# Tying gathers to the instruction queue of VectorE: a mark and a copy, or a pass over the gathers' own index columns

## The chip, the cores and the metric

The kernel runs on one core of a Trainium2 chip. The core has five engines with a queue each, which run side by side and wait for one another through semaphores: TensorE (PE in the profile, its weight loads PEld), VectorE (DVE), ScalarE (ACT), GpSimd (POOL) and SyncE (SP), which here only issues transfers. The metric is the device time of one launch in microseconds. Three runs before the change took 3876.13, 3902.46 and 3901.21 us; their median is 3901.21 us. The execution that was profiled took 3892.48 us, with a span of 3890.7 us.

## The reference

There are 16 graphs of 1024 nodes with 64 channels, and a weighted 1024 by 1024 adjacency for each, with some 16 neighbours to a node. Four graph layers follow one another, each applied to `relu(layernorm(x))` and added to `x`. Layers 0, 1 and 3 are matrix products with the adjacency and small weights. Layer 2 is the one that matters here: it thins the neighbourhood of every node by a rule on the ranks of its neighbours, and takes, for every node and channel, a weighted sum of three quantiles over the neighbours that are left:

```python
vals = where(valid[..., None], x[:, None, :, :], big)
sv = sort(vals, axis=2)                      # over the neighbours of a node
for tau, wt in zip([0.25, 0.5, 0.75], [0.25, 0.5, 0.25]):
    pos = clip(tau * (m - 1), 0)             # m neighbours
    lo, hi, frac = floor(pos), ceil(pos), pos - floor(pos)
    agg = agg + wt * (gather(lo) * (1 - frac) + gather(hi) * frac)
```

Two small products, a relu and the node mask follow.

## The kernel before

**Stages.** The function `direct_path` is cut into streams, which are Python generators over the 16 graphs. `adjacency` loads a graph, transposes it on TensorE and makes sort keys of the neighbours. `neighbour_lists` reads the keys back, sorted by the number of neighbours, and takes from each row the largest eight again and again (line 1111 and lines 1120 to 1127), until it has a list of row numbers for every node. `layers` does layers 0 and 1 and stores the rows of layer 2 in DRAM, as `h_d`. `gathers` fetches, for each place of each list, one row of 64 numbers per node. `sorts` runs a sorting network over the fetched rows on VectorE (line 1316) and forms the weighted sum (lines 1333 and 1335). `tail` fetches the results back into the order of the nodes (line 1355) and does the rest.

**Batches and groups.** The 1024 nodes of a graph are ordered by their number of neighbours and cut into eight batches of 128, one node to a partition. `PLACES` gives the number of places of each batch, 21 down to 11, and `LISTS` the length of its list in the tile `index`, 40 down to 16 columns; the lists lie one behind another. `GROUPS` takes the batches in five groups: the first two batches alone, the others in pairs, whose rows lie side by side in one tile `raw`, so that one step of the network sorts both. The few long lists of the first batch are packed and fetched separately (line 1264).

**Gathers.** A gather is one indirect transfer that GpSimd prepares: 128 rows of `h_d`, chosen by one column of `index`, into one place of `raw` (line 1283). There are 124 of them for a graph, 1984 in all. GpSimd works through its queue in order; apart from the gathers it has only the key loads (line 1096), the packed rows and the results to fetch, and the gate's copies.

**The order.** All is emitted by hand in one pass over the streams, under a plan: a `Clock` holds estimated times of the engines, each stream says by `yield` at what estimated VectorE time it wants to go on, and the loop at the end of the function takes the next stream whose time has come. So the order of the instructions in every queue is fixed when the program is built. The plan counts 1.39 us for a gather, and lets GpSimd's clock run 5 us ahead of VectorE's at most (`yield clk.pool - 5` after every four gathers).

**The gate.** That the plan puts a gather at some point of VectorE's work doesn't hold GpSimd back: its queue is its own. The function `gate` (lines 919 to 925) ties the two. At every fourth gather, and before the key loads of a graph, VectorE writes one element of `slots` (a memset, line 922), and GpSimd copies that element to `opened` (line 924). The copy waits for the memset, and what stands behind the copy in GpSimd's queue waits with it. A gate is left out when the last one lies less than 3 us back on the plan's clock. The profile has 477 of them.

Of the kernel before, what the change touches and what calls it, by code (L numbers as in the profile page):

```python
# [7 lines left out]
F32 = mybir.dt.float32  # L8
# [6 lines left out]
ALU = mybir.AluOpType  # L15
AX = mybir.AxisListType

P = 128
C = 64
NB = 8  # L20
N = 1024
# [12 lines left out]
I16 = mybir.dt.int16  # L34
# [21 lines left out]
PLACES = [21, 19, 17, 16, 15, 13, 12, 11]  # L56
PACKS, NPACK = [(0, 0, 21, 2, 64), (1, 0, 23, 1, 32), (1, 32, 24, 4, 24), (2, 0, 28, 10, 12)], 3

LISTS = [40, 24, 24, 16, 16, 16, 16, 16]
KB = 4  # L60


# [62 lines left out]
def _program(cap, low, above, homes):  # L125

    home, out = [0] * cap, []
    for layer, flips in zip(_network(cap, low, above), homes.split(), strict=True):  # L130
        pairs = sorted({(home[i], home[j]) for i, j, _, _ in layer})
        steps, moved = ([], []), []
        for (s, u), flip in zip(pairs, flips, strict=True):
            some = [c for c in layer if (home[c[0]], home[c[1]]) == (s, u)]
            for greater in (True, False):
                moves = flip in ("bi" if greater else "bj")
                to = (s if greater else u) ^ moves
                for first, dims in _patterns([(i, j) for i, j, a, b in some if (a if greater else b)]):
                    steps[0 if moves else 1].append((greater, s, u, to, first, dims))
                moved += [c[0 if greater else 1] for c in some if moves]  # L140
        for e in moved:
            home[e] ^= 1
        out += steps[0] + steps[1]
    return out, [(home[q], q, e) for e, q in enumerate(_wanted(cap, low))]
# [587 lines left out]
def direct_path(ctx: ExitStack, tc: tile.TileContext, t: dict, out: bass.AP, flag):  # L732
# [3 lines left out]
    nc = tc.nc  # L736
# [84 lines left out]
    clk = Clock()  # L821
# [90 lines left out]
        return v.rearrange("c (q u p) -> c u q p", u=2, p=P)[:, u]  # L912


    marks = []
    slots = const.tile([1, 8], F32, name="mark")
    opened = const.tile([1, 2], F32, name="gate")

    def gate():
        if not marks or clk.dve > marks[-1] + 3.0:  # L920
            k = len(marks)
            nc.vector.memset(slots[:, k % 8:k % 8 + 1], 0.0)  # L922
            clk.dve += 0.15
            nc.gpsimd.tensor_copy(opened[:, k % 2:k % 2 + 1], slots[:, k % 8:k % 8 + 1])  # L924
            marks.append(clk.dve)


    state = [dict() for _ in range(B)]
    done = set()
    queued = []  # L930
# [156 lines left out]
    def neighbour_lists(b):  # L1087


        g = state[b]  # L1090
        ks = []

        def load_keys(i):
            if i < NB:
                k = lists.tile([P, N], F16, name="k", bufs=KB)
                nc.gpsimd.indirect_dma_start(k, None, g["keys_d"],
                                             bass.IndirectOffsetOnAxis(ap=g["node"][:, i:i + 1], axis=0))
                clk.pool = max(clk.pool, clk.dve) + 1.3
                ks.append((k, clk.pool + 3.5))

        gate()
        for i in range(KB):
            load_keys(i)
        total = sum(LISTS)
        found = lists.tile([P, total], F32, name="found", bufs=1)
        m = g["m"]
        o = 0
        for i in range(NB):
            src, at = ks[i]
            yield at  # L1110
            nc.vector.max(out=found[:, o:o + 8], in_=src)  # L1111
            clk.dve += 1.15
            yield clk.dve
            less, before = src.bitcast(I16), None
            for r in range(1, LISTS[i] // 8):


                least = found[:, o + 7:o + 8]
                if r == 1:
                    ts(less, src, least, None, op0=ALU.subtract)  # L1120
                else:
                    ts(less, less, before, least, op0=ALU.add, op1=ALU.subtract)
                before = least
                most = nodes.tile([P, 8], U16, name="most")
                nc.vector.max(out=most, in_=less.bitcast(U16))  # L1125
                o += 8
                ts(found[:, o:o + 8], most.bitcast(I16), 0.0, least, op0=ALU.min, op1=ALU.add)
                clk.dve += 1.8
                yield clk.dve
            o += 8  # L1130
            load_keys(i + KB)
        index = lists.tile([P, total], I32, name="index")
        to, of = (v.rearrange("p (s u) -> p u s", u=2) for v in (index, found))
        none = lists.tile([P, total // 2], F32, tag="far", name="none", bufs=1)
        nc.vector.tensor_copy(to[:, 1], of[:, 1])
        ts(none, of[:, 0], 0.0, float(N + 1), op0=ALU.is_equal, op1=ALU.mult)
        tt(to[:, 0], none, of[:, 0], ALU.add)
        pack_d = dram.tile([NPACK, P], I32, name="pack_d")
        pack = nodes.tile([P, NPACK], I32, name="pack")
        for l, p0, s0, ns, nn in PACKS:  # L1140
            nc.sync.dma_start(pack_d[l, p0:p0 + ns * nn].rearrange("(n s) -> n s", s=ns), index[:nn, s0:s0 + ns])
        for l, size in enumerate(sizes):
            nc.sync.dma_start(pack[:size, l:l + 1], pack_d[l, :size].rearrange("(n o) -> n o", o=1))

        s = nodes.tile([P, 2, NB], F32, name="s")
        tt(s[:, 0], m, cap8, ALU.is_gt)
        tt(s[:, 1], m, low8, ALU.is_lt)
        tt(s[:, 0], s[:, 0], s[:, 1], ALU.max)
        tt(bad, bad, s[:, 0], ALU.max)


        above = nodes.tile([P, 2, NB], I32, name="above")
        ts(above[:, 0], m, 1.0, None, op0=ALU.add)
        ts(above[:, 1], above[:, 0], 1, None, op0=ALU.arith_shift_right)
        tt(s[:, 0], half8, above[:, 1], ALU.subtract)
        ts(s[:, 1], m, -1.0, None, op0=ALU.add)
        at = nodes.tile([P, 3, NB], F32, name="at")
        for k in range(3):
            nc.vector.scalar_tensor_tensor(at[:, k], s[:, 1], (k + 1) / 4, s[:, 0], op0=ALU.mult, op1=ALU.add)
        far = lists.tile([P, 3, QT], F32, name="far", bufs=1)  # L1160
        o, e = 0, E_Q
        for b0, n, cap, low, *_ in GROUPS:
            k = len(_wanted(cap, low))
            tt(far[:, :, o:o + k * n].rearrange("p t (q i) -> p t q i", i=n),
               cf[:, None, e:e + k, None].to_broadcast([P, 3, k, n]),
               at[:, :, None, b0:b0 + n].to_broadcast([P, 3, k, n]), ALU.subtract)
            o, e = o + k * n, e + k
        act(far, far, AF.Abs)
        for k, w in enumerate((0.25, 0.5, 0.25)):
            act(far[:, k], far[:, k], AF.Relu, bias=wcol[:, k:k + 1], scale=-w)  # L1170
        g.update(index=index, pack=pack)
        done.add(("index", b))
        yield after(1.7, act=1.7)
        while b >= 2 and ("sorts", b - 2) not in done:
            yield None
        wts = lists.tile([P, QT], F32, name="wts", bufs=2)
        tt(wts, far[:, 0], far[:, 2], ALU.add)
        tt(wts, wts, far[:, 1], ALU.add)
        clk.dve += 0.4
        g.update(wts=wts)  # L1180
        done.add(("lists", b))
# [65 lines left out]
    def gathers(b):  # L1247
        g = state[b]
        yield max(g["rows_at"], clk.pool)
        for k, (b0, n, cap, *_) in enumerate(GROUPS):  # L1250
# [15 lines left out]
                    clk.pool += 1.39  # L1266
                rows_d = dram.tile([NPACK, P, C], F32, name="rows_d")
            for s in range(cap):
                if s % (4 // n) == 0:
                    gate()  # L1270
                if k == 0 and s == 9:
                    for l, size in enumerate(sizes):
                        nc.sync.dma_start(rows_d[l, :size], packed[:size, l * C:(l + 1) * C])
                if k == 0 and s == 17:
                    for l, p0, s0, ns, nn in PACKS:
                        nc.sync.dma_start(raw[:nn, s0:s0 + ns, :],
                                          rows_d[l, p0:p0 + ns * nn].rearrange("(n s) c -> n s c", s=ns))
                for i in range(n):
                    if s >= PLACES[b0 + i]:
                        continue  # L1280
                    clk.pool += 1.39
                    at = sum(LISTS[:b0 + i]) + s
                    nc.gpsimd.indirect_dma_start(raw[:, s, i * C:(i + 1) * C], None, h_ds[b % 3],  # L1283
                                                 bass.IndirectOffsetOnAxis(ap=g["index"][:, at:at + 1], axis=0))
                if (s + 1) % (4 // n) == 0:
                    yield clk.pool - 5
# [128 lines left out]
    nc.vector.memset(none[:, :1], BIG)  # L1415
    nc.vector.memset(none[:, 1:], 0.0)
    sizes = [max(p0 + ns * nn for l, p0, _, ns, nn in PACKS if l == k) for k in range(NPACK)]
    programs = [_program(*group[2:]) for group in GROUPS]
    edge = lists.tile([1, 2, C], F32, tag="ab", name="edge")
    nc.vector.memset(edge[:, 0], 0.0)  # L1420
# [169 lines left out]
```

## Time and profile before

| what | before |
|---|---|
| median of three runs | 3901.21 us |
| span of the profiled execution | 3890.7 us |
| VectorE busy | 3040.5 us, 78% |
| GpSimd busy | 2650.6 us, 68% |
| TensorE busy | 2010.3 us, 52% |
| ScalarE busy | 1424.2 us, 37% |
| gathers, line 1283 | 1984, 2151.8 us |
| the gate's copies, line 924 | 477, 162.7 us |
| the gate's memsets, line 922 | 477, 27.5 us |

The profile gives for each engine the time in which it did something. A group of instructions is given as a line of the code, an engine, an operation, the tiles written and read, the count, the busy time and the mean duration of one, and the idle time of the engine just before such an instruction, with what ended it ("issue" means that nothing was waited for that the profile shows). The chain of waits is followed back from the last instruction, at each step to what released it. In the lists of instructions in order of time, the first number is the start in us, the second the duration.

### The profile page before, as it was taken

What the parts mean: (1) busy time and instruction counts of PE and PEld (TensorE: products, weight loads), DVE (VectorE), ACT (ScalarE), POOL (GpSimd) and SP (SyncE); (2) the same over time, 40 slices, a digit from 0 to 9 for tenths busy, and PEclk for the clock granted to TensorE, in tenths of its full rate; (3) what the DMA queues carried; (4) which work ended last, traced back from release to release, by engine and by line L of the source; (5) the groups of instructions that cost most, each with busy time, mean ns of one, the idle gap of its engine ahead of it and who ended that gap; (6) DMA issues with size and microseconds to landing.
All of it is one profiled execution on the core that took longest, in us unless ns stands there. A gap on an engine that the chain in (4) does not pass through costs nothing.

```text
span 3890.7 us, 30892 instructions
## 1 busy us (share of the span) xinstructions
PE 2010.3 (52%) x7587; PEld 934.0 (24%) x7587; DVE 3040.5 (78%) x7345; ACT 1424.2 (37%) x2786; POOL 2650.6 (68%) x2792
## 2 busy tenths in 40 slices
PE   6463463746554474645546565565457545641113
PEld 3222221223222222222222222232222212220101
DVE  2557877969787897888788798989699867979572
ACT  5444343244443434333342444343444424330000
POOL 1077565867767776776767677777778776777781
PEclk8676666667676686666666676767667666765555
DMA  2313233152423425233341525242343424232121
GB/s 89 124 40 117 48 98 114 47 166 53 153 64 94 121 65 152 69 114 79 86 126 48 172 54 163 58 156 56 100 119 108 113 52 126 65 105 59 43 52 55
DMA packets 237343, 362.37 MB, mean 93 GB/s; under 512 B 126848, under 2 KB 128496, under 8 KB 237152
## 3 DMA queue, kind: packets, MB, share of 16 engines
q1 hardware_dynamic: 156912, 255.00, 19.0%
q0 software_dynamic: 80096, 104.70, 13.5%
q8 instruction: 62, 1.02, 0.1%
q14 instruction: 129, 1.06, 0.1%
q10 hardware_dynamic: 144, 0.59, 0.0%
HBM read 245.30 MB, written 114.81 MB: 93 GB/s over the span
## 4 chain that ended last, share of the span: by engine, by line
DVE 42%; issue 16%; POOL 10%; PE 10%; another core or an unknown queue 9%; ACT 9%; DMA 4%; SPq 0%; DVEq 0%; ACTq 0%; POOLq 0%
DVE other L1316 11%; DVE raw L1316 10%; POOL raw L1283 8%; DVE most L1125 5%; PE pt L882 4%; DVE found L1111 2%; DVE agg L1335 2%; ACT adjt L1220 2%; ACT sink L1055 2%; DVE k L1120 1%; DMA k<-keys_d,node 1%; POOL res L1355 1%; PE pt L906 1%; DVE nb L947 1%
## 5 line engine op out<-in xcount | busy, mean ns | idle before, releaser
L1283 POOL DMA_INDIRECT raw<-h_d,index x1984 | 2151.8, 1085 | 558.9 <-issue 532.6
L1316 DVE TENSOR_TENSOR other<-raw 128x512 f32<-128x512 f32 (+11 forms) x816 | 536.8, 688 | 152.0 <-DMA raw<-h_d,index 103.6
L882 PE MATMUL pt<-adjt,ha 128*65 128x512 f32 (+1 forms) x1024 | 489.7, 640 | 63.0 <-DVE ha L1207 27.1
L924 POOL COPY gate<-mark 1x1 f32<-1x1 f32 x477 | 162.7, 341 | 409.4 <-DVE mark L922 372.6
L994 PE MATMUL pt<-eh,nbt 128*128 128x512 f16 (+3 forms) x1024 | 238.3, 381 | 322.1 <-ACT nbt L983 256.1
L954 PE MATMUL pt<-ef,a 128*128 128x128 f32 x1024 | 212.5, 367 | 294.9 <-issue 112.4
L1316 DVE TENSOR_TENSOR raw<-other 128x512 f32<-128x512 f32 (+10 forms) x464 | 355.8, 791 | 5.3
L1125 DVE MAX8 most<-k 128x8 uint16<-128x1024 uint16 x208 | 255.4, 1228 | 10.9 <-DVE k L1120 3.3
L954 PEld LDWEIGHTS pt<-ef,a 128*128 128x128 f32 x1024 | 163.4, 190 | 383.8 <-issue 186.6
L1032 ACT ACTIVATE nb<-pt 128x1024 f16<-128x1024 f32 x128 | 130.6, 1021 | 328.7 <-remote 169.3
L955 ACT COPY adjt<-pt 128x512 f32<-128x512 f32 x256 | 140.3, 585 | 282.6 <-remote 148.0
L882 PEld LDWEIGHTS pt<-adjt,ha 128*65 128x65 f32 (+1 forms) x1024 | 149.2, 149 | 386.3 <-issue 375.3
L1028 PE MATMUL pt<-eh,gone 128*128 128x128 f16 x1024 | 128.7, 255 | 181.9 <-DVE gone L1006 90.6
L1316 DVE TENSOR_TENSOR raw<-other,raw 128x640 f32<-128x640 f32 (+3 forms) x448 | 216.5, 494 | 6.7 <-remote 1.8
L994 PEld LDWEIGHTS <-nbt 128*128 128x128 f16 x1024 | 111.2, 121 | 452.8 <-ACT nbt L983 286.0
L1316 DVE TENSOR_TENSOR raw<-raw,other 128x128 f32<-128x128 f32 (+7 forms) x496 | 211.6, 436 | 6.1
L883 ACT COPY big<-pt 64x1024 f32<-64x1024 f32 (+1 forms) x32 | 32.2, 1008 | 502.5 <-PE pt L882 299.3
L961 ACT ACTIVATE nb<-nb 128x512 f16<-128x512 f16 x256 | 159.7, 629 | 147.7 <-DVE nb L947 53.8
L1392 PE MATMUL tm<-at,ha 128*64 128x512 f32 x512 | 176.8, 794 | 67.0 <-DMA at<-adjt_d 59.1
L1316 DVE TENSOR_TENSOR other<-other,raw 128x128 f32<-128x128 f32 (+4 forms) x448 | 201.6, 461 | 4.5 <-DVE other L1316 0.3
L1001 ACT ACTIVATE gone<-pt,sf 128x512 f16<-128x512 f32 x256 | 161.6, 685 | 104.7 <-remote 35.1
L1111 DVE MAX8 found<-k 128x8 f32<-128x1024 f16 x128 | 156.4, 1222 | 42.5 <-DMA k<-keys_d,node 42.4
(189 smaller groups left out, 4249.3 us busy)
## 6 DMA issues: line engine op xcount, KB each, us to landing
a<-in_adj_dram SPq DMA_DIRECT2D x64, 1024.0 KB
adjt_d<-adjt SPq DMA_DIRECT2D x64, 1024.0 KB
at<-adjt_d SPq DMA_DIRECT2D x128, 512.0 KB
keys_d<-nb SPq DMA_DIRECT2D x64, 512.0 KB
raw<-h_d,index POOLq DMA_INDIRECT x1984
x<-in_x_dram SPq DMA_DIRECT2D x16, 256.0 KB
h_d<-h SPq DMA_DIRECT2D x16, 256.0 KB
agg_d<-agg SPq DMA_DIRECT2D x16, 256.0 KB
```

Source lines behind the costliest of these rows:

```text
L882: nc.tensor.matmul(p[p0:p0 + n, s], h[:, j, :n], adjt[:, j, s], start=j == 0, stop=j == NB - 1)
L924: nc.gpsimd.tensor_copy(opened[:, k % 2:k % 2 + 1], slots[:, k % 8:k % 8 + 1])
L954: nc.tensor.transpose(p[:, u * P:(u + 1) * P], a[:, j * P:(j + 1) * P], identf)
L955: nc.scalar.copy(adjt[:, 4 * q:4 * q + 4, i * P:(i + 1) * P], p.rearrange("p (u m) -> p u m", m=P))
L961: act(nb[:, i, s], nb[:, i, s], AF.Copy, accum_out=mn[:, q, i:i + 1])
L994: nc.tensor.matmul(p[:, o:e], nbt[:, j, :], stair[:, :e - o], start=j % 4 == 0, stop=j % 4 == 3 and j != i)
L1001: act(gone[:, i, s], p[:, s], AF.Abs, bias=sf[:, 2 + q, i:i + 1], scale=2.0)
L1111: nc.vector.max(out=found[:, o:o + 8], in_=src)
L1125: nc.vector.max(out=most, in_=less.bitcast(U16))
L1283: nc.gpsimd.indirect_dma_start(raw[:, s, i * C:(i + 1) * C], None, h_ds[b % 3], bass.IndirectOffsetOnAxis(ap=g["index"][:, at:at + 1], axi ...
L1316: tt(view(two[to], *((i, vi) if greater else (j, vj)), w), view(two[s], i, vi, w), view(two[u], j, vj, w), ALU.max if greater else ALU.min)
L1392: nc.tensor.matmul(p[q * C:(q + 1) * C, :], ha[:, j, :], even(ats[j], q), start=j == 0, stop=j == NB - 1)
```

## The change

The gate goes away: no memset, no copy, no `slots`, no `opened`, and nothing in front of the key loads. In its place the wait is put on what the gather reads anyway. Before every four gathers VectorE adds zero, in place, to the four columns of `index` that these gathers will read. A gather reads its column, so it waits for the pass, without an instruction of its own on GpSimd. A pass is made for every four gathers; the rule of 3 us is gone.

For that the four columns must lie side by side. In a paired group four gathers in a row are two places of two batches, so the lists of paired batches are now interleaved, place by place; `FIRST` gives where a group begins. The lists are written with a stride of two there, the row numbers are turned into integers in two parts (single batches and pairs) in place of one, and `found`, which now has gaps where the shorter list of the first pair ends, is set to zero once and kept.

```diff
+FIRST = [0, 40, 64, 112, 144, 176]
...
-    def gate():
-        if not marks or clk.dve > marks[-1] + 3.0:
-            k = len(marks)
-            nc.vector.memset(slots[:, k % 8:k % 8 + 1], 0.0)
-            clk.dve += 0.15
-            nc.gpsimd.tensor_copy(opened[:, k % 2:k % 2 + 1], slots[:, k % 8:k % 8 + 1])
-            marks.append(clk.dve)
...
-        gate()
         for i in range(KB):
             load_keys(i)
...
+            k, n = next((k, n) for k, (b0, n, *_) in enumerate(GROUPS) if b0 <= i < b0 + n)
+            first = FIRST[k] + (i - GROUPS[k][0])
+            eights = [found[:, e:e + 7 * n + 1:n] for e in range(first, first + LISTS[i] * n, 8 * n)]
...
-                ts(found[:, o:o + 8], most.bitcast(I16), 0.0, least, op0=ALU.min, op1=ALU.add)
+                ts(eights[r], most.bitcast(I16), 0.0, least, op0=ALU.min, op1=ALU.add)
...
-        nc.vector.tensor_copy(to[:, 1], of[:, 1])
-        ts(none, of[:, 0], 0.0, float(N + 1), op0=ALU.is_equal, op1=ALU.mult)
-        tt(to[:, 0], none, of[:, 0], ALU.add)
+        for e, z, n in ((0, FIRST[2], 1), (FIRST[2], total, 2)):
+            to, of = (v[:, e:z].rearrange("p (s u i) -> p u s i", u=2, i=n) for v in (index, found))
+            less = none[:, e // 2:z // 2].rearrange("p (s i) -> p s i", i=n)
+            nc.vector.tensor_copy(to[:, 1], of[:, 1])
+            ts(less, of[:, 0], 0.0, float(N + 1), op0=ALU.is_equal, op1=ALU.mult)
+            tt(to[:, 0], less, of[:, 0], ALU.add)
...
-                if s % (4 // n) == 0:
-                    gate()
+                if s % (4 // n) == 0 and s < PLACES[b0]:
+
+                    some = g["index"][:, FIRST[k] + s * n:FIRST[k] + s * n + 4]
+                    ts(some, some, 0, None, op0=ALU.add)
+                    clk.dve += 0.15
...
-                    at = sum(LISTS[:b0 + i]) + s
+                    at = FIRST[k] + s * n + i
...
+    found = const.tile([P, FIRST[-1]], F32, name="found")
+    nc.vector.memset(found, 0.0)
```

More of the change, by code (lines that the diff above doesn't have):

```diff
@@ L912, in even @@
         return v.rearrange("c (q u p) -> c u q p", u=2, p=P)[:, u]
-    marks = []
-    slots = const.tile([1, 8], F32, name="mark")
-    opened = const.tile([1, 2], F32, name="gate")
-    def gate():
-        if not marks or clk.dve > marks[-1] + 3.0:
-            k = len(marks)
-            nc.vector.memset(slots[:, k % 8:k % 8 + 1], 0.0)
-            clk.dve += 0.15
-            nc.gpsimd.tensor_copy(opened[:, k % 2:k % 2 + 1], slots[:, k % 8:k % 8 + 1])
-            marks.append(clk.dve)
     state = [dict() for _ in range(B)]
@@ L1099, in load_keys @@
                 ks.append((k, clk.pool + 3.5))
-        gate()
         for i in range(KB):
             load_keys(i)
-        total = sum(LISTS)
-        found = lists.tile([P, total], F32, name="found", bufs=1)
+        total = FIRST[-1]
         m = g["m"]
-        o = 0
         for i in range(NB):
             src, at = ks[i]
+            k, n = next((k, n) for k, (b0, n, *_) in enumerate(GROUPS) if b0 <= i < b0 + n)
+            first = FIRST[k] + (i - GROUPS[k][0])
+            eights = [found[:, e:e + 7 * n + 1:n] for e in range(first, first + LISTS[i] * n, 8 * n)]
             yield at
-            nc.vector.max(out=found[:, o:o + 8], in_=src)
+            nc.vector.max(out=eights[0], in_=src)
             clk.dve += 1.15
@@ L1115, in neighbour_lists @@
             for r in range(1, LISTS[i] // 8):
-                least = found[:, o + 7:o + 8]
+                least = eights[r - 1][:, 7:8]
                 if r == 1:
@@ L1125, in neighbour_lists @@
                 nc.vector.max(out=most, in_=less.bitcast(U16))
-                o += 8
-                ts(found[:, o:o + 8], most.bitcast(I16), 0.0, least, op0=ALU.min, op1=ALU.add)
+                ts(eights[r], most.bitcast(I16), 0.0, least, op0=ALU.min, op1=ALU.add)
                 clk.dve += 1.8
                 yield clk.dve
-            o += 8
             load_keys(i + KB)
         index = lists.tile([P, total], I32, name="index")
-        to, of = (v.rearrange("p (s u) -> p u s", u=2) for v in (index, found))
         none = lists.tile([P, total // 2], F32, tag="far", name="none", bufs=1)
-        nc.vector.tensor_copy(to[:, 1], of[:, 1])
-        ts(none, of[:, 0], 0.0, float(N + 1), op0=ALU.is_equal, op1=ALU.mult)
-        tt(to[:, 0], none, of[:, 0], ALU.add)
+        for e, z, n in ((0, FIRST[2], 1), (FIRST[2], total, 2)):
[4 more added lines that the diff above has]
+            tt(to[:, 0], less, of[:, 0], ALU.add)
         pack_d = dram.tile([NPACK, P], I32, name="pack_d")
```

## The prediction, made before the result was known

> **What bounds the kernel now.** I read the page from the top: busy shares, then the chain of waits, then the groups and the waits of GpSimd.
>
> ```profile
> PE 2010.3 (52%) x7587; PEld 934.0 (24%) x7587; DVE 3040.5 (78%) x7345; ACT 1424.2 (37%) x2786; POOL 2650.6 (68%) x2792
> ...
> DVE 42%; issue 16%; POOL 10%; PE 10%; another core or an unknown queue 9%; ACT 9%; DMA 4%; SPq 0%; DVEq 0%; ACTq 0%; POOLq 0%
> ...
> L1283 POOL DMA_INDIRECT raw<-h_d,index x1984 | 2151.8, 1085 | 558.9 <-issue 532.6
> ...
> L924 POOL COPY gate<-mark 1x1 f32<-1x1 f32 x477 | 162.7, 341 | 409.4 <-DVE mark L922 372.6
> ```
>
> VectorE is the backbone: 78% busy, and the largest part of the chain. No engine is full, so the end is set by VectorE's work plus its waits. GpSimd comes second. Its 162.7 us of copies look like a prize of 4% of the span, and the 372.6 us in front of them like another. Neither is one as it stands: the 372.6 us is the waiting that the gate is there to cause, and it will stand before the gathers instead (124.2 us of it is the lead-in before the first keys). What the 162.7 us are worth, the order of time shows.
>
> ```profile
> 1005.10 0.95 POOL L1283 DMA_INDIRECT raw<-h_d,index  x1 [0.31 <-issue]
> ...
> 1006.05 0.18 POOL L924 COPY gate<-mark 1x1 f32<-1x1 f32 x1
> ...
> 1006.39 0.97 POOL L1283 DMA_INDIRECT raw<-h_d,index  x1 [0.16 <-issue]
> ...
> 1007.66 0.95 POOL L1283 DMA_INDIRECT raw<-h_d,index  x1 [0.30 <-issue]
> ```
>
> Two gathers in a row lie 0.30 us apart even with nothing between. A copy starts at once behind a gather, runs in that gap, and the next gather follows 0.16 us later. With VectorE idle the gate so lengthens the gap from 0.30 to 0.34 us only. Over the whole trace, 392 of the 477 copies start without a wait, and the gap around them has a mean of 0.489 us, against 0.307 us between gathers.
>
> **How far GpSimd reaches the end.** What VectorE waited for:
>
> ```profile
> DVE stat L858 <- ACT mid L856: 105.6, 11, 36.3
> DVE other L1316 <- DMA raw<-h_d,index: 103.6, 13, 25.8
> ...
> DVE found L1111 <- DMA k<-keys_d,node: 42.4, 9, 9.1
> ```
>
> Gathers hold the sorts up for 103.6 us in 13 places, key loads hold up the lists for 42.4 us. Walking the chain piece by piece, 295 gathers and 77 of the 477 copies lie on it. A copy starts on average 4.3 us after its mark: GpSimd is mostly behind its ties, and reaches the end of a group too late in some graphs only.
>
> [...] The trace agrees for copies: 0.18 us with MAX8 running on VectorE, a mean of 0.53 us when they met an `other<-raw` sort step. Gathers take 0.952 us beside an idle VectorE and 1.148 us beside sort steps. VectorE loses next to nothing: its sort steps are 0.006 us over their floor with or without a gather beside them, and small integer passes that met a gather took 0.17 us mostly, 0.4 us at the worst, never a whole gather. [...] two independent passes of 0.17 us each start 0.08 us apart (1023.90 and 1023.98).
>
> **The change, part by part.** I start from 3893 us, the mean of the four times known (3876.13, 3902.46, 3901.21, 3892.48), since the median stands at the upper end of them.
>
> Copies gone. 392 gaps shrink from 0.489 to 0.307 us: 392 x 0.182 = 71 us. At the 85 copies that did wait, the gather now waits itself; the copy (0.18 us or more) drops out, some 0.2 us each, 17 us. Together 88 us of GpSimd's queue. On the chain lie 77 copies: 77 x 0.19 = 15 us. The other copies lie where GpSimd afterwards waits for VectorE anyway.
>
> Passes in place of memsets. The built programs have 544 passes for 477 memsets. No 4-column integer pass stands in the trace. The nearest row is this, and its neighbours have 190 and 192 ns:
>
> ```profile
> L971 DVE TENSOR_SCALAR si<-si 128x8 int32<-128x8 int32 x16 | 2.9, 182 | 0.5
> ```
>
> A pass will thus be listed at 0.17 to 0.19 us, some 100 us of busy time in all. What it costs the queue is less. A memset (0.06 us, here at 1001.21) slips into the bubble between two dependent sort steps:
>
> ```profile
> 1000.77 0.49 DVE L1316 TENSOR_TENSOR raw<-raw 128x320 f32<-128x320 f32 x1
> 1001.21 0.06 DVE L922 MEMSET mark<- 1x1 f32 x1
> 1001.30 0.43 DVE L1316 TENSOR_TENSOR raw<-other,raw 128x256 f32<-128x256 f32 x1
> ```
>
> The step behind it starts 0.04 us after the one before it ended, as it does without a memset. Over all sort steps, the gap from end to next start is -0.042 us without and -0.011 us with a memset, so a memset costs 0.03 us. For a pass the bounds are 0.03 us and the listed 0.185 us; I take 0.05, since a pass is independent of both neighbours, and the next may start 0.08 us behind it. That is 544 x 0.05 - 477 x 0.03 = 13 us, with ends at 2 and 86 us. Behind a pass in the queue stand sort steps and list steps, but it waits for nothing: its columns were made by VectorE long before; only one pass in a graph also waits for the transfers that read the packed columns, issued many microseconds earlier.
>
> A pass may also hold a gather up. Gathers beside a sort step and a `tensor_scalar` took 1.271 us against 1.148 us, those beside MAX8 and a `tensor_scalar` 0.983 us; I take 0.05 us for each of 544, 27 us of GpSimd's queue, which leaves 61 of its 88 us, and by the same share of the chain 10 of the 15 us.
>
> Lists. Three conversions (0.214, 0.199, 0.248 us) become six smaller ones at about 0.2 us: 0.54 us more, 9 us over 16 graphs. The stride of two in results of eight columns I cost at nothing[...]. The one memset of `found` lies in the lead-in.
>
> Sum: VectorE's queue +22 us. Its share on the end lies between 42% (chain) and 78% (busy): 9 to 17 us, I take 13. GpSimd -10 us. That gives +3 us, 3896; of the rest, the better fit with the plan, which counts 5.56 us for four gathers where 4 x 1.085 + 3 x 0.307 + 0.489 = 5.75 us were needed (now about 5.6), should take away some of the 103.6 us of late gathers; 13 places at 0.5 us are about 7 us. I put the end at 3889 us, 0.3% under the median.
>
> **Rivals.**
> *GpSimd paces more than the chain shows.* The chain follows one last waiter; gathers that end sooner also free transfers and key loads sooner. If all 61 us reach the end and VectorE pays 10: 3893 - 61 + 10 = 3842. For it: GpSimd's lag of 4.3 us and the plan's deficit of 0.19 us for every four gathers. Against it: 85 gates at which GpSimd stood still, where what it has saved is given back.
> *Passes cost what they are listed at.* 86 + 9 = 95 us on a queue that is the backbone; all of it on the path, less 10: 3978; with half on the path, 3930. I work with 3945. For it: the passes carry 128 partitions and raise a semaphore each. Against it: the 0.08 us between independent passes.
> *The order.* The other VectorE instructions stand in another order at 311 places of the built program, key loads and result fetches move by some four gathers, and 67 more ties hold gathers that were free before. Four gathers are 5.6 us; if half the graphs lose them once: +45 us, 3935. The same shift may gain as much.
>
> **Numbers.** Within 1% of 3901 (3862 to 3940) as worked out: 0.45. GpSimd paces, or the order gains: 0.32, at 3842. The two slow rivals: 0.23 together, at 3935 to 3945. Range: 3825 leaves out only a gain beyond the first rival, 3950 the passes at nearly full price.
>
> **What will show it.** Right: GpSimd's busy time falls by about the copies' 163 us less some lengthening of gathers, to some 2500 us; the gap before a fourth gather is 0.30 us; passes are listed near 0.18 us and VectorE's busy time rises by 40 to 80 us; VectorE's waits for gathers stay at 70 to 110 us. Wrong: passes of 0.5 us or more[...], gathers at 1.15 us or more on average, or a wait before a pass; then it is slower. If the waits for gathers and keys, 146 us together, fall under 80 us, the first rival is right.

## The result, and the profile after

The changed kernel took 3998.35 us (median of 4 runs, 3985.07 to 4009.79), the kernel before 3889.51 us (4 runs, 3876.13 to 3902.46). The ratio is 1.0279, with a 95% interval of 1.0222 to 1.0336: 2.8% slower, and outside the predicted range. Ratios, here and below, are formed from the fast runs alone (at most 1.5% above the kernel's fastest), and can differ by up to 0.9% from the quotient of two medians. The profiled execution has a span of 4008.0 us.

The lines of the page that answer to those of before (busy shares; chain of waits; the gathers; below them, from the list of groups, the pass):

```profile
PE 2038.4 (51%) x7587; PEld 941.9 (23%) x7587; DVE 3077.1 (77%) x7461; ACT 1425.0 (36%) x2786; POOL 2463.3 (61%) x2315
...
DVE 40%; PE 16%; another core or an unknown queue 13%; ACT 11%; issue 10%; DMA 5%; POOL 4%; SPq 0%; DVEq 0%; ACTq 0%; POOLq 0%
...
L1274 POOL DMA_INDIRECT raw<-h_d,index x1984 | 2127.1, 1072 | 1091.2 <-issue 525.4
```

```profile
L1260 DVE TENSOR_SCALAR index<-index 128x4 int32<-128x4 int32 x544 | 89.5, 176 | 0.0
```

Every single item of the change came out about as small as it was priced. The 544 passes are listed at 176 ns, GpSimd has 187 us less to do, VectorE 37 us more, and a gather takes 1072 ns, where it took 1085. GpSimd's part of the chain fell from 10% to 4%. What grew is the rest: TensorE's part from 10% to 16%, and from 9% to 13% the part that the profile gives to "another core or an unknown queue". There is no other core here; it is time for which the profile finds no releaser. In the list of waits the same thing is called "remote". ScalarE's longest waits in the changed kernel (in total, times, longest):

```profile
ACT big L884 <- PE pt L883: 350.3, 24, 19.7
ACT nb L1020 <- remote: 252.0, 34, 20.0
ACT adjt L943 <- remote: 205.4, 36, 13.7
...
ACT big L884 <- remote: 126.7, 5, 29.7
```

Before, the second and third of these were smaller:

```profile
ACT nb L1032 <- remote: 169.3, 22, 23.3
ACT adjt L955 <- remote: 148.0, 28, 18.5
ACT mid L892 <- remote: 138.8, 6, 109.6
```

The instructions of the first two lines read what TensorE has accumulated, and where their releaser is unnamed they wait for TensorE's semaphore alone. And here is GpSimd in order of time, with a tie in front of every fourth gather:

```profile
606.36 0.94 POOL L1274 DMA_INDIRECT raw<-h_d,index  x1 [0.30 <-issue]
607.61 0.95 POOL L1274 DMA_INDIRECT raw<-h_d,index  x1 [0.31 <-issue]
608.86 0.95 POOL L1274 DMA_INDIRECT raw<-h_d,index  x1 [0.30 <-issue]
610.12 1.17 POOL L1274 DMA_INDIRECT raw<-h_d,index  x1 [0.31 <-issue]
```

A tie that is met in time can't be seen: the gathers stand 0.30 us apart from first to last. Why TensorE's part of the chain grew as well is not settled.

### The profile page after: what moved, and what is told of

Same layout as the page of the kernel before. It is cut to its first block, busy times and chain, and to the rows that moved or that the text cites. A ratio compares the mean times of both kernels' runs of the same rounds, so it can differ in the third digit from the quotient of the medians.

```text
span 4008.0 us, 30568 instructions
## 1 busy us (share of the span) xinstructions
PE 2038.4 (51%) x7587; PEld 941.9 (23%) x7587; DVE 3077.1 (77%) x7461; ACT 1425.0 (36%) x2786; POOL 2463.3 (61%) x2315
## 4 chain that ended last, share of the span: by engine, by line
DVE 40%; PE 16%; another core or an unknown queue 13%; ACT 11%; issue 10%; DMA 5%; POOL 4%; SPq 0%; DVEq 0%; ACTq 0%; POOLq 0%
DVE other L1307 10%; DVE raw L1307 10%; PE pt L883 7%; DVE most L1113 4%; ACT adjt L1208 3%; POOL raw L1274 3%; DVE found L1099 2%; DVE agg L1326 2%; ACT sink L1043 2%; DMA raw<-h_d,index 1%; PE pt L907 1%; DVE k L1108 1%; PE pt L1016 1%; ACT pt L1023 1%
## 5 line engine op out<-in xcount | busy, mean ns | idle before, releaser
L1274 POOL DMA_INDIRECT raw<-h_d,index x1984 | 2127.1, 1072 | 1091.2 <-issue 525.4
L1307 DVE TENSOR_TENSOR other<-raw 128x512 f32<-128x512 f32 (+11 forms) x816 | 538.2, 688 | 146.3 <-DMA raw<-h_d,index 89.8
L1084 POOL DMA_INDIRECT k<-keys_d,node x128 | 135.8, 1061 | 200.5 <-DVE node L1069 133.2
L1011 PE MATMUL pt<-nb,eh 128*128 128x512 f16 x256 | 130.3, 509 | 164.4 <-ACT pt L1023 122.0
L1016 PE MATMUL pt<-eh,gone 128*128 128x128 f16 x1024 | 137.1, 268 | 143.7 <-DVE gone L994 55.0
```

The costliest lines, as they stand in the source:

```text
L1016: nc.tensor.matmul(p[:, d], gone[:, j, i * P:(i + 1) * P], big_i, start=False, stop=j == 4 * q + 3 and i // 4 != q)
L1084: nc.gpsimd.indirect_dma_start(k, None, g["keys_d"], bass.IndirectOffsetOnAxis(ap=g["node"][:, i:i + 1], axis=0))
L1307: tt(view(two[to], *((i, vi) if greater else (j, vj)), w), view(two[s], i, vi, w), view(two[u], j, vj, w), ALU.max if greater else ALU.min)
```

## The experiments

The theories, at first: the time was lost by the new order; or by the passes as work of VectorE; or because the pass is a worse tie than the copy. Later ones are named where they come up.

Eighteen kernels were run, in five groups; the kernels of a group share a chip and their runs of the kernel before, whose median was 3883, 3892, 3898, 3834 and 3662 us in the five. So ratios are compared, and those of the last group with each other only. The first and the last group ran on the same chip. "Unnamed waits" are ScalarE's waits over 0.5 us for which the profile names no releaser, added up over its list in order of time: 588 us before, 750 us after. (The expectations say 606 for the kernel before; one wait had been counted twice there.)

The total counts whole waits, not only the part that is late. In the kernel before, one of them is nearly all a true wait, the 109.6 us of `mid` above: TensorE itself stood still for 97.6 us until the results were fetched, and ended the matmuls that `mid` reads at 3644.8 us; `mid` started at 3648.35. Without it the kernel before has 478 us. Four of the kernels below have the same wait (111 to 115 us) among their unnamed ones, and their totals without it stand in brackets; in the others it has a name or counts as "issue".

In all kernels "in the order of before", every other instruction of VectorE, ScalarE, GpSimd and SyncE stands where it stood in the kernel before, but for the conversions of the lists and the one memset of `found` where a kernel has the change's lists.

### Order or tie

The pass in the old order, mark and copy in the new one, and neither in both orders (of the edits, the lines that matter):

```diff
 # passes, old order: the plan counts as the gate did, before the key loads too
+                if s % (4 // n) == 0:
+                    gate()               # advances the plan's clock only
...
                     ts(some, some, 0, None, op0=ALU.add)
-                    clk.dve += 0.15
 # mark and copy, new order: a gate wherever the change has a pass, none before the key loads
-        if not marks or clk.dve > marks[-1] + 3.0:
...
-                if s % (4 // n) == 0:
+                if s % (4 // n) == 0 and s < PLACES[b0]:
                     gate()
 # no tie: the changed kernel, the plan counting as after it or as before
-                    ts(some, some, 0, None, op0=ALU.add)
```

> The changed kernel (passes, interleaved lists, no gate), but with the plan's clock advanced as the gate advanced it, so that every other instruction stands in the order of before in each queue. Theory ORDER (the other order costs the 109 us): about the time of before, 3880 to 3900 us. Theory TIES (544 passes in place of 477 marks, tied more tightly or dearer on VectorE, cost it): about the time after, 3980 to 4010 us.

> The kernel before, with a mark and a copy at exactly the 544 places of the passes, 0.15 us of plan for each and none before the key loads, so that every other instruction stands in the order of after. Theory ORDER: 3990 to 4020 us, as after or a little more, since the copies lengthen GpSimd's queue. Theory TIES by the pass itself: 3880 to 3920 us. Theory TIES by their number: near 4000 us as well.

> The changed kernel without the passes; the plan still counts 0.15 us for each, so the order is that of after. Gathers wait for their row numbers and for their place in raw alone. Theory ORDER: near 4000 us (3970 to 4020), whatever the tie. Theory TIES: 3870 to 3920 us, since what holds the gathers is gone.

> The changed kernel without passes, in the order of before: no tie of any kind. Theory ORDER: 3870 to 3900 us, as before. Theory TIES: the same or faster, 3850 to 3890 us. If a tie is of use in itself (it keeps gathers from running ahead), slower than before in either, some 3950 us.

| kernel | ratio to before | 95% interval | unnamed waits, us |
|---|---|---|---|
| passes, old order | 1.0177 | 1.0121 to 1.0232 | 678 (565) |
| mark and copy, new order | 1.0124 | 1.0070 to 1.0177 | 567 |
| no tie, new order | 1.1905 | 1.1818 to 1.1991 | 1077 |
| no tie, old order | 1.2049 | 1.1989 to 1.2110 | 1379 |

None of the four times was expected: the first two lie between the theories, and the kernels without ties lie 600 us and more above anything that was foreseen. Both halves cost, and they add up: 1.8% for the pass in the copy's place and 1.2% for the order, against 2.8% together. (The kernel with copies in the new order has 67 copies more than the kernel before and no gate ahead of the key loads, so its 1.2% is not the order alone; the changed kernel and the one with passes in the old order have the same passes, and their ratios, though from two groups, lie 1.0% apart.) Where the order's share shows is in two of VectorE's waits. In the old order, with copies or with passes, it waits 14.4 and 19.0 us for `m` before it makes `node`; in the new order with copies:

```profile
DVE other L1314 <- DMA raw<-h_d,index: 132.4, 17, 25.7
DVE node L1080 <- ACT m L1077: 46.4, 4, 18.1
```

With passes, the new order likewise has 49.4 us for `m` (19.0 in the old), and 89.8 us for gathers (61.5 in the old). That is some 30 us for each of the two waits, in both pairs, against some 50 us that the order costs.

The last two kernels show what happens without a tie, and what the unnamed waits are. The kernel without ties, in the old order, has this chain:

```profile
DVE 40%; another core or an unknown queue 26%; ACT 10%; issue 10%; PE 9%; DMA 2%; POOL 2%; SPq 0%; DVEq 0%; ACTq 0%; POOLq 0%
```

One such wait, from TensorE's and ScalarE's lists in order of time. TensorE's matmuls of line 883 end at 220 us; the copy that waits for them and for nothing else starts at 275.76:

```profile
213.44 6.60 PE L883 MATMUL pt<-adjt,ha 128*64 128x512 f32 x15
```

```profile
275.76 1.01 ACT L884 COPY big<-pt 64x1024 f32<-64x1024 f32 x1 [63.94 <-remote]
```

In all this time GpSimd sent gathers without a break, at 1.25 us each:

```profile
220.52 0.95 POOL L1281 DMA_INDIRECT raw<-h_d,index  x1 [0.30 <-issue]
221.77 0.95 POOL L1281 DMA_INDIRECT raw<-h_d,index  x1 [0.30 <-issue]
...
274.24 0.95 POOL L1281 DMA_INDIRECT raw<-h_d,index  x1 [0.31 <-issue]
275.49 0.95 POOL L1281 DMA_INDIRECT raw<-h_d,index  x1 [0.30 <-issue]
```

Of other traffic there is none in these 56 us, from 220 to 276 (the queues' packets, megabytes and share, and what was issued):

```profile
q0 software_dynamic: 1386, 1.42, 11.1%
...
raw<-h_d,index POOLq DMA_INDIRECT x45
```

ScalarE went on some 55 us after the matmuls that it waited for had ended. What is late is the signal, not ScalarE: the trace has TensorE's update of the semaphore only at 275.73 us, and all of the 94 unnamed waits of the changed kernel end within 0.08 us of such an update. That ScalarE waited for instructions instead has no sign in the trace. Over the whole span of the kernel before, the page lists 191 packets of the kind `instruction`:

```profile
q8 instruction: 62, 1.02, 0.1%
q14 instruction: 129, 1.06, 0.1%
```

In the list for these 56 us there are none. (Which engine such packets are for, the page doesn't say.) From here on the late signal is called lateness. The kernel before has smaller cases of it, the first at 238.02 us, about 15 us after its matmuls:

```profile
208.83 13.95 PE L882 MATMUL pt<-adjt,ha 128*64 128x512 f32 x32
```

```profile
238.02 1.01 ACT L883 COPY big<-pt 64x1024 f32<-64x1024 f32 x1 [28.33 <-remote]
```

### What in a tie ends the lateness

```diff
 # beats: no tie, old order, at each of the 544 places
+                        nc.gpsimd.memset(beat_t[:, k % 2:k % 2 + 1], 0.0)     # one element
 # long beats: the same with ten memsets of 128 by 64
 # passes and beats: passes in the old order and the one-element memset
 # three copies: the kernel before, each gate's copy made three times
+            for _ in range(3):
                 nc.gpsimd.tensor_copy(opened[...], slots[...])
```

> No tie, order of before, but at each of the 544 places GpSimd makes a one-element memset of its own that waits for nothing outside GpSimd. In the run without ties the other engines notice semaphores late (2 to 64 us) while GpSimd prepares gathers in an unbroken row. Theory BREAK (any GpSimd instruction that isn't a gather ends that): 3880 to 3950 us, since the beats break the rows as the gate's copies did. Theory PAUSE (only time in which GpSimd prepares nothing ends it; a beat takes 0.1 us): 4600 to 4700 us, as without.

> As the last, but with ten memsets of 128x64 at each place[...]. Theory BREAK: no better than one small beat, and slower by what GpSimd is longer busy: 4000 to 4150 us. Theory PAUSE: far faster than 4677 us, 4000 to 4200 us, where the small beat is not. If neither breaks nor pauses matter but only being held back to VectorE's work: 4700 us or more.

> Passes in the order of before (3947 us) and in addition the one-element memset on GpSimd at each of the 544 places. Theory BREAK: back to the time of before, 3870 to 3900 us, though GpSimd does more. Theory PAUSE: 3940 to 3970 us, unchanged or slower.

> The kernel before with each gate's copy made three times, so that a gate lasts about 1.2 us instead of 0.5 us. Theory PAUSE: the longer stop in the row helps the others and costs GpSimd some 0.8 us x 477 = 380 us, of which 420 us of waiting take most: 3850 to 3930 us. Theory BREAK: one copy was enough, so only the cost is left: 3920 to 4050 us.

| kernel | ratio to before | 95% interval | unnamed waits, us |
|---|---|---|---|
| no tie, beats | 1.1980 | 1.1897 to 1.2062 | 1240 |
| no tie, long beats | 1.1552 | 1.1505 to 1.1599 | 2 |
| passes and beats, old order | 1.0190 | 1.0140 to 1.0240 | 785 (673) |
| three copies at each gate | 1.0154 | 1.0106 to 1.0201 | 93 |

That any other instruction between gathers ends the lateness falls: a beat of 0.09 us hides in the 0.30 us that lie between two gathers anyway (mean gap with a beat 0.32 us), and changes nothing. Time between gathers does end it. With long beats, and nearly so with three copies (mean gap 1.32 us), ScalarE's unnamed waits are gone. The times of these two missed what PAUSE expected (4496 us against 4000 to 4200, 3952 against 3850 to 3930; by its time alone, the second fits BREAK); it is the waits that decide between the theories. Both kernels are slow for another reason. The chain of the one with three copies (GpSimd has 52% in the other):

```profile
POOL 54%; DVE 18%; issue 17%; DMA 5%; PE 3%; ACT 3%; another core or an unknown queue 1%; SPq 0%; POOLq 0%; DVEq 0%; ACTq 0%
```

GpSimd itself has become the bound. So there are two costs: with pauses too short the signals come late (1240 us of unnamed waits at a mean gap of 0.32 us); with pauses too long GpSimd paces (52% and 54% of the chain). Where lateness was present, no pause that was tried beat that of the kernel before.

### VectorE's share, the lists, and pauses for the pass

```diff
 # passes and three copies: passes in the old order, at each place
+                        for _ in range(3): nc.gpsimd.tensor_copy(beat_b[...], beat_a[...])   # waits for nobody
 # lists: the change's lists and conversions, but the gate of before
 # spare passes: the kernel before, and at each place
+                        ts(spare_columns, spare_columns, 0, None, op0=ALU.add)               # read by nobody
 # three copies at every second gate
+            for _ in range(1 + 2 * (k % 2)):
                 nc.gpsimd.tensor_copy(opened[...], slots[...])
```

> The passes as ties in the order of the kernel before, and at each pass three GpSimd copies of one element that wait for nobody: pauses between gathers as in the kernel with three copies per gate, where ScalarE's waits without a named releaser fell from 606 to 93 us. ROWS (the pass costs time because it takes the pauses out of the gathers): those waits fall below 200 us (678 with passes alone), and the time is that of three copies at gates, 3950 (3925 to 3975), no more than that although VectorE carries the passes. VECTORE (the pass costs time as VectorE's own work): 3950 and the 40 to 65 us of passes on top, 3990 to 4020.

> Only the interleaved lists, with their six conversions instead of three and the tables cut from them; mark and copy as before, order as before. ROWS: 3885 to 3905, since the rows of gathers are unchanged. VECTORE: 3 more instructions for each of 32 groups' sets, some 10 us, 3895 to 3905. LAYOUT (the scattered writes and strided reads of the lists cost more than their busy time): 3920 or more.

> The kernel before, with 544 passes over four columns of a table that nobody reads, in VectorE's queue where the tie's passes would be; mark and copy still tie the gathers. ROWS: the passes lie in VectorE's slack for the most part and the pauses stay, 3890 to 3915. VECTORE: the passes' 45 to 50 us come on top nearly whole, 3930 to 3945.

> The kernel before with three copies at every second gate, one at the others. ROWS: a pause of 0.8 us after every eight gathers or so is enough for ScalarE's unnamed waits to fall below 250 us (606 before, 93 with three at each), while GpSimd gains half of the 290 us of copies: 3870 to 3915, below or near the kernel before. LINEAR (the copies only lengthen GpSimd's queue): half of the 60 us that three at each gate cost, 3920 or more.

| kernel | ratio to before | 95% interval | unnamed waits, us |
|---|---|---|---|
| passes and three copies | 1.0586 | 1.0538 to 1.0633 | 0 |
| lists alone | 1.0017 | 0.9993 to 1.0041 | 612 (497) |
| spare passes alone | 0.9990 | 0.9967 to 1.0013 | 464 |
| three copies at every second gate | 1.0044 | 1.0006 to 1.0081 | 361 |

The lists cost nothing that can be measured, and 544 passes in VectorE's queue cost nothing either: VectorE's work isn't what the change lost. The first kernel missed both its expectations, 4118 us. Its unnamed waits are gone as expected, but GpSimd's part of the chain is 22%: a gather with a tie of its own starts 0.43 us after the last of the three copies on average, one without 0.16 to 0.18, so that the pauses were 1.54 us long, at 544 places instead of 477. With three copies at every second gate the time fits the expectation; the unnamed waits fell less than expected there (below 250).

### The pause alone

What is left is the short pause. In the kernel before, the gap around a copy that needn't wait has a mean of 0.49 us; with the pass it is 0.31. Three kernels change only that, in the order of before:

```diff
 # passes and one copy: at each pass
+                        nc.gpsimd.tensor_copy(beat_b[...], beat_a[...])      # waits for nobody
 # memset at gates: the kernel before, tie kept
-            nc.gpsimd.tensor_copy(opened[:, k % 2:k % 2 + 1], slots[:, k % 8:k % 8 + 1])
+            nc.gpsimd.memset(slots[:, k % 8:k % 8 + 1], 0.0)
 # passes, three copies at every third pass
+                        for _ in range(3 if k % 3 == 0 else 0): nc.gpsimd.tensor_copy(beat_b[...], beat_a[...])
```

> The passes as ties in the order of the kernel before, and one GpSimd copy of one element at each pass that waits for nobody. PAUSE (what the pass took away is the short pause that the copy made between gathers): ScalarE's unnamed waits fall from 678 below 600 us, and the time from 3947 to 3885 to 3925, although GpSimd has 544 instructions more. KIND (a gather that itself waits for VectorE is the worse tie, or GpSimd's queue counts): 3945 or more, as with passes alone or with a beat of 0.09 us, 3972.

> The kernel before with GpSimd's copy of the mark replaced by GpSimd's one-element memset of the mark, which waits for VectorE in the same way; a beat of that kind took 0.09 us and left a gap of 0.30 us between gathers, where the copy leaves 0.34 to 0.75. PAUSE: the gathers stand closer, ScalarE's unnamed waits rise above 650 us, and the time goes to 3920 to 3960. KIND: the tie is as before and GpSimd's queue is shorter, 3875 to 3900.

> The passes as ties in the order of the kernel before, and at every third pass three GpSimd copies that wait for nobody: a pause of 1.2 us after every twelve gathers or so, as the kernel with three copies at every pass shows it. PAUSE: ScalarE's unnamed waits below 400 us (678 with passes alone), 3890 to 3925 against 3947 with passes alone, although GpSimd has some 250 us more to do. KIND: 3950 to 4000.

| kernel | median, us | ratio to before | 95% interval | unnamed waits, us |
|---|---|---|---|---|
| passes and one copy | 3831.25 | 1.0000 | 0.9981 to 1.0019 | 364 |
| memset at gates | 3904.48 | 1.0171 | 1.0132 to 1.0210 | 636 (526) |
| passes, three copies at every third | 3839.52 | 1.0013 | 0.9991 to 1.0035 | 324 |

The kernel before took 3834 us in this group, some 55 us less than when the expectations were written; as ratios all three times fit PAUSE. The unnamed waits of the kernel with the memset do not quite: they are 636 us, and more than 650 were expected.

The memset waits for VectorE's mark just as the copy did, but takes 0.11 us on average, and the gap around it is 0.31 us:

```profile
702.42 1.06 POOL L1282 DMA_INDIRECT raw<-h_d,index  x1 [0.31 <-issue]
703.48 0.09 POOL L923 MEMSET mark<- 1x1 f32 x1
703.78 1.95 POOL L1282 DMA_INDIRECT raw<-h_d,index  x1 [0.22 <-issue]
```

That alone makes the kernel before 1.7% slower, as much as the pass does. And the pass with an idle copy beside it is as fast as the kernel before, although GpSimd has 544 instructions more than with the pass alone (which was not run in this group; its ratio was 1.018 in the first):

```profile
603.06 0.95 POOL L1104 DMA_INDIRECT k<-keys_d,node  x1 [0.30 <-issue]
604.01 0.18 POOL L924 COPY beat_b<-beat_a 1x1 f32<-1x1 f32 x1
604.35 0.96 POOL L1296 DMA_INDIRECT raw<-h_d,index  x1 [0.16 <-issue]
```

ScalarE's waits of the kernel with the memset, and then of that with passes and one copy:

```profile
ACT nb L1031 <- remote: 139.6, 28, 17.3
ACT adjt L954 <- remote: 138.3, 24, 15.0
```

```profile
ACT nb L1040 <- remote: 93.3, 12, 21.1
...
ACT adjt L963 <- remote: 76.1, 13, 11.6
```

Between these two, on one chip and in one order, unnamed waits differ by 272 us, 162 without the true wait near the end, and the time by 73 us. So taking the pause away costs what the pass cost, and giving it back to the pass makes good the loss: that the pause is what the pass took away is shown, and that the kind of tie is worse falls.

### Pauses without ties, and the change with a copy

```diff
 # no tie, old order, at each of the 544 places one copy, or three, that wait for nobody
+                        nc.gpsimd.tensor_copy(beat_b[...], beat_a[...])
 # the changed kernel and one such copy beside each pass
```

> No ties, the order of the kernel before, three GpSimd copies that wait for nobody at each of the 544 places. PAUSES ALONE (a tie does no more than break the rows of gathers): the time of three copies at gates, a ratio of 1.01 to 1.04 to the kernel before. TIES TOO (gathers that run ahead of the plan cost time by themselves, by the place they take in buffers and queues): 1.08 or more, though ScalarE's unnamed waits are gone.

> No ties, the order of the kernel before, one GpSimd copy that waits for nobody at each of the 544 places. PAUSES ALONE: 1.00 to 1.04. TIES TOO: 1.15 to 1.20, near the 1.198 of the beats of 0.09 us.

> The changed kernel with one GpSimd copy beside each pass that waits for nobody. PAUSE: the order's 1.2% stays and the pause's 1.6% goes, a ratio of 1.008 to 1.017, like the copies as ties in this order (1.0124). If the new order needs another pause, or the sum of the two was chance: 1.02 or more.

| kernel | median, us | ratio to before | 95% interval | unnamed waits, us |
|---|---|---|---|---|
| no tie, three copies | 3974.66 | 1.0856 | 1.0838 to 1.0874 | 0 |
| no tie, one copy | 3623.33 | 0.9898 | 0.9881 to 0.9914 | 0 |
| changed kernel and one copy | 3697.06 | 1.0093 | 1.0076 to 1.0110 | 0 |

In this group the kernel before took 3662 us (7 runs, 3658 to 3668) where it had taken 3834 to 3898, on the very chip of the first group, where it took 3883. None of the three kernels has an unnamed wait, though in other groups kernels with one copy at each place have 364 and 567 us of them. There is no profile of the kernel before from this group, but its time speaks for the same: the lateness, which the other groups have, was absent here. So, although the ratios 1.0856 and 1.0093 fall where TIES TOO and PAUSE put them (0.9898 lies under both ranges), they settle neither, and this group can't say whether pauses make ties needless where lateness is present. With three copies GpSimd has 54% of the chain, as it had with three copies at each gate. The group says two other things. Without lateness the changed kernel with its pauses back is still 0.9% slower; since lists and passes cost nothing in the third group, this is the order or the 67 more copies. For the order speaks that the same number of copies cost nothing in the old order, with passes (1.0000, in the fourth group) and without ties (0.9898, here). And without lateness the ties are no help: the kernel without them, with one copy at each place, was 1.0% faster than the kernel before, the only one that measurably beat it.

## Why the prediction was wrong

**Right.** The sizes of what was priced item by item. Passes were forecast at 0.17 to 0.19 us and take 0.176; GpSimd's busy time at some 2500 us is 2463; VectorE's rose by 37 us, just under the 40 to 80 forecast; the gap before a fourth gather is 0.30 us; VectorE's waits for gathers, forecast at 70 to 110 us, are 89.8. That passes hide beside sort steps and that the lists cost nothing is shown by the kernels that have them alone (ratios 0.999 and 1.002). None of the three signs that were to mean "slower" came: no pass of 0.5 us (the longest took 0.42), no gathers of 1.15 us on average (1.072), no wait before a pass (0.0 us in the list). The time went where none of the signs looked.

**The step that failed: "Copies gone".** It counted 88 us of GpSimd's queue as won, 10 of them on the path. The queue did win, and VectorE did have it: in the old order with passes its waits for gathers fell from 103.6 to 61.5 us, those for keys from 42.4 to 18.1:

```profile
DVE other L1317 <- DMA raw<-h_d,index: 61.5, 8, 18.1
...
DVE found L1109 <- DMA k<-keys_d,node: 18.1, 6, 5.7
```

Together that is 79.6 us (110.7 in the changed kernel itself), just under the 80 that was to mean that the rival "GpSimd paces" is right. Yet that kernel is 1.8% slower, some 70 us. The copies' 0.18 us of longer gap was not idle cost: it kept lateness down, and the kernel before with the gap alone shortened, from 0.49 to 0.31 us, is 1.7% slower. The sign of the term was wrong, about -10 us forecast and about +70 measured. The chain of before showed where to look, 9% of the span with no named releaser, and the prediction has no term for it: it was put at nothing without a reason.

**The second step: the "better fit with the plan", -7 us.** The new order costs 1.2% with copies, some 50 us (1.0% with passes; 0.9% with the copies beside passes where there is no lateness). That is the rival "The order", worked out at 3935 us with one loss of four gathers in half the graphs; in size it was right, by luck, since half the graphs was a guess, and the mechanism only in part, since half of what shows are waits for `m`, not for gathers. It was put among cases with a chance of 0.23 for two together, and should have had a place in the sum. The two failed steps, +70 and +50 us on 3890, give 4010; measured were 3998.

**Open.** Why a dense row of gathers goes with late semaphores of other engines is not settled. In one order, unnamed waits go with pauses in every group that has them at all, but the total over ScalarE doesn't convert to time at a fixed rate: at the time of the kernel before there are 478 us without the true wait (497 with the lists, 464 with the spare passes), but also 324 to 364 us. In the last group they were absent at gaps at which other groups have them, on a chip that had them in the first group, so there is a second condition that these runs don't show. Nor do they tell a pause from a lower rate of gathers: long pauses at fewer places (361 and 324 us) did about as much as a short one at each (364). Whether pauses without ties would win where lateness is present stays open: with copies they ran in the last group only, and with long beats GpSimd was the bound.

## What to carry to other kernels

An instruction that seems to be overhead in a queue of gathers may be doing a second job by the gap that it leaves (here 0.49 us against 0.31, worth 1.7%): before taking it away, replace it by one of the same wait and a shorter duration and look at the other engines' waits, above all those without a named releaser. A change that touches a planner's clock is two changes, the edit and a new order; build the edit with the old order first, and price the order as a term of the sum (here 1.2% with copies). And where the chain has a tenth of unnamed time (here 9%), no sum over named items bounds the result; but before that time is added up, the longest of its waits have to be looked at one by one, since a true wait can be among them (here 109.6 of 588 us).

## What the runs showed of the hardware

- GpSimd's indirect transfers in dense rows (0.95 us each, 0.30 us apart) go together with late semaphores of TensorE: 15 us and 55 us after its matmuls in the two cases shown. With a tie at every fourth gather or so, in the old order, ScalarE's unnamed waits without the one true wait are 565 us at a mean gap of 0.31 us, 478 us at 0.49 us, 93 us at 1.32 us and none at 1.54 us, each from another group.
- A one-element GpSimd memset of 0.09 us between two gathers leaves the gap at 0.30 to 0.32 us. A one-element copy takes 0.18 us at the least, 0.30 to 0.34 us on average and now and then over 1 us, and makes the gap 0.47 to 0.49 us on average.
- A gather with a wait of its own on VectorE, though long met, starts 0.43 us (mean; often 0.52) after three GpSimd copies, one without such a wait 0.15 to 0.18 us; behind a single copy, one with such a wait starts after 0.16 us in the case shown. Behind another gather both start after 0.30 us.
- The same kernel took 3662 us in one group of runs and 3834 to 3898 us in four others, one of them on the same chip; no kernel profiled in the first has unnamed waits.
